# A two-layer graph network with residual and normalisation: rows of x split by way of a PSUM bank, VectorE's instructions in program order in the setup, and earlier due times for the last blocks

## The chip, the cores and the metric

The kernel runs on one core of one Trainium2 chip. The metric is device time in microseconds of one execution, the median over several runs; the profile is of one further execution.

## The reference

The inputs are x (12,500 nodes of 256 features, float32), 200,000 edges (src, dst), sorted by dst, and the weights of two graph layers and of an output layer. The edges are not spread evenly: dst is 12,500 times the square of a uniform number, so the low nodes have many edges and the high ones few.

```python
def _sage_conv(x, src, dst, W_l, b_l, W_r):
    msgs = x[src]
    agg = jax.ops.segment_sum(msgs, dst, num_segments=N_NODES)
    deg = jax.ops.segment_sum(jnp.ones((src.shape[0],), x.dtype), dst, num_segments=N_NODES)
    mean = agg / jnp.maximum(deg, 1.0)[:, None]
    return mean @ W_l + b_l + x @ W_r
...
    h = jax.nn.relu(_sage_conv(x, src, dst, W1_l, b1, W1_r))
    h = jax.nn.relu(_sage_conv(h, src, dst, W2_l, b2, W2_r))
    return h @ W3 + b3
...
    x = _layernorm(x + _L0_gnn_ref(x, edge_index, ...), axis=-1)
```

## The kernel before

**Two ways to sum the messages.** The 12,500 nodes make 98 blocks of 128 rows, and the 200,000 edges make 1,563 tiles of 128. For the "hot" nodes (the first 5 x 256 in layer 1, the first 7 x 256 in layer 2) the kernel counts how often each source occurs for each target (`count`, L677) and multiplies the count matrix with all rows of the table (`product`, L654). The rows are float32 and the products bf16, so each row is split in three bf16 parts that add up to it: `x3_d` holds the parts of x, `h3_d` those of layer 1's output h. For the "cold" nodes the rows of the edges' sources are gathered from memory: one gather (L257) is an indirect DMA of 128 rows, issued by GpSimd (POOL), and four gathers make a round. TensorE (PE) sums the round's rows by a one-hot matrix (the strips, `part_ps`, L269), ScalarE (ACT) copies the sum out (`some`, L279), a second small product places it (`sum_ps`, L285), and VectorE (DVE) adds it to a ring of eight blocks of sums (L299). Four buffers `got` hold the rows of four rounds, so POOL can be at most four rounds ahead of the strips.

**Stages.** The setup (L301 to L546) loads src and dst, turns them edge by edge into the tables that the gathers and the one-hot matrices need, and tests the data against what the plan of the program assumes. `by_sorting` is a slower program that runs if a test fails; the branch is taken at the very end (L45), by a flag that is written to memory (L988) and loaded again (L41). Layer 1 has 269 rounds (1,076 gathers from x), layer 2 has 247 (988 gathers from h).

**The order.** The order on PE and POOL is written out by hand (`manual_schedule`, L445); the framework's scheduler orders the instructions of DVE, ACT and SP. `layer` (L584) does it: in each round it issues four gathers and their strips, adds what the round before gave, and in three parts of the round works on finished blocks (`pieces`) and on the dense work (`fill`). The dense work has estimated costs, and `due` (L623) spreads it over all rounds but the last eight. In layer 1 its first stage is the count of the first 256 nodes together with the split of x (`splits`, L803, one `split_rows` for each of the 98 blocks); after it come the products of the groups, each beside the count of the next. A block of 128 nodes is finished when all edges that can fall into it have been summed; `left_after` (L236) tells it from `at_least` (L94), which allows the data to be SLACK = 8 tiles from the square law. A finished block goes to a queue, where at most two are worked on, in three pieces in layer 1 (`first_block`, L913) and five in layer 2 (`last_block`, L939), two turns apart. The blocks of a dense group go to the same queue when its product is done (L800).

**The split before.** `split_rows` (L648) loads a block of x, and `exact` (L637) makes the parts: DVE subtracts the upper bf16 half of x from x (L643, into `rest`), and the upper half of the rest from the rest (L644, the third part); ACT copies the two upper halves (L645, L646); SP stores the three parts (L652). All of it lies in SBUF. `exact` is also used for h in `first_block` (L935).

Of the kernel before, what the change touches and what calls it, by code (L numbers as in the profile page):

```python
# [7 lines left out]
F32 = mybir.dt.float32  # L8
# [15 lines left out]
P = 128  # L24
# [3 lines left out]
def kernel(tc, x, src, dst, w1l, b1, w1r, w2l, b2, w2r, w3, b3, out):  # L28

    args = (x, src, dst, w1l, b1, w1r, w2l, b2, w2r, w3, b3, out)
    flag = tc.nc.dram_tensor("unfit_d", (1, 1), I32).ap()
    by_runs(tc, *args, flag)
    with tc.tile_pool(name="flag", bufs=1) as pool:
        unfit_i = pool.tile([1, 1], I32, name="unfit_i")  # L40
        tc.nc.sync.dma_start(unfit_i, flag)  # L41
        unfit = tc.nc.values_load(
            unfit_i[0:1, 0:1], min_val=0, max_val=1,
            skip_runtime_bounds_check_because="it is clamped to 0..1 where it is made")
    with tc.If(unfit > 0):  # L45
        by_sorting(tc, *args)
# [3 lines left out]
def by_runs(  # L50
# [36 lines left out]
    FAR = 1 << 20  # L87
    SLACK = 8
    RB = 8
    RN = RB * P  # L90
    assert D % P == 0 and E % 2 == 0 and G * W == P


    def at_least(t):  # L94
        return N * (max(t - SLACK, 0) / NT) ** 2 - 2

    def at_most(t):
        return N * ((t + SLACK) / NT) ** 2 + 2

# [201 lines left out]
    with tc.tile_pool(name="setup", bufs=1) as su, \  # L301
            tc.tile_pool(name="setup_ps", bufs=2, space=PSUM) as su_ps:
        def edges(a, first, name, fill):
# [14 lines left out]
            return t  # L318

        src_i = edges(src, 0, "src_i", 0)  # L320
        dst_i = edges(dst, 0, "dst_i", FAR)
# [9 lines left out]
        whole = (NT // G) * G  # L331
        with nc.allow_non_contiguous_dma(reason="one edge of each tile"):
            nc.scalar.dma_start(f4_i[:, :NT // G], dst[0:whole * P].rearrange(
                "(g j l) -> j g l", j=G, l=P)[:, :, 0])
            if NT > whole:
                left = NT - whole
                nc.scalar.dma_start(
                    f4_i[0:left, NT // G:NG],
                    dst[whole * P:whole * P + (left - 1) * P + 1:P][:, None])
            nc.scalar.dma_start(f8_i, dst[lows[HG1] * P:PAIRS * P].rearrange(  # L340
                "(g j l) -> j g l", j=G, l=2 * P)[:, :, 0])
            nc.scalar.dma_start(f1_i, dst[None, 0:HC * P * P:P])
            nc.scalar.dma_start(fours_i, dst[0:P * P:P * G][:, None, None].to_broadcast([P // G, G, 1]))
            for c in range(C0, PAIRS // P):
                nc.scalar.dma_start(pair_i[:, c:c + 1], dst[c * P * P:(c + 1) * P * P:2 * P][
                    :, None, None].to_broadcast([P // 2, 2, 1]))

# [15 lines left out]
        nc.vector.tensor_copy(lanes_5[:, :, :LW // 5], steps_f[:, :LW].rearrange("p (a b) -> p a b", a=5))  # L363
        nc.vector.tensor_copy(steps_7[:, :, :NB // 7], steps_f[:, :NB].rearrange("p (a b) -> p a b", a=7))


# [65 lines left out]
        nc.vector.tensor_copy(within_f, within)  # L432
        nc.vector.tensor_scalar(lo2, after, within_f, None, op0=OP.add)

        for g in got:

            nc.vector.memset(g[:, :, D:D + 1], 1.0)
        nc.vector.memset(sums, 0.0)
        nc.vector.memset(degs, 0.0)
        nc.vector.memset(ones, 1.0)  # L440
        nc.vector.memset(ones_b, 1.0)
        nc.vector.memset(zeros_b, 0.0)

# [13 lines left out]

        nc.vector.tensor_copy(steps, steps_f)
        bits = su.tile([P, HC, P], I32, name="bits")
        low = su.tile([P, HC, P], F32, name="low")  # L460
        nc.vector.tensor_scalar(bits, src_i[:, :HC], P - 1, None, op0=OP.bitwise_and)
        nc.vector.tensor_copy(low, bits)
# [4 lines left out]
        start = su.tile([P, HC], F32, name="start")  # L467
        nc.vector.tensor_copy(start[:, 0:1], fours_i)
        nc.vector.tensor_copy(start[:, 1:], first[:, 1:HC])
        f1 = su.tile([1, HC * P], F32, name="f1")  # L470
        nc.vector.tensor_copy(f1, f1_i)
        off_f = su.tile([1, HC * P], F32, name="off_f")
        nxt_first = su.tile([P, HC], F32, name="nxt_first")
        nc.vector.tensor_copy(nxt_first, nxt_i[:, :HC, P - 1])
        most_c = max(b - a for a, b in spans)
# [20 lines left out]
        nxt_f = su.tile([P, CH, P], F32, name="nxt_f")  # L496
        nc.vector.tensor_copy(nxt_f, nxt_i)
        nc.vector.scalar_tensor_tensor(scr, dst_f, 0.0, nxt_f, op0=OP.add, op1=OP.is_gt,
# [10 lines left out]
        for sign in (-1, 1):  # L509
            law = su.tile([1, NG], F32, name="law", bufs=2)  # L510
            nc.vector.tensor_scalar(law, fours, float(G) / NT, float(sign * SLACK) / NT,
                                    op0=OP.mult, op1=OP.add)
            nc.vector.tensor_scalar(law, law, 0.0, None, op0=OP.max)
# [69 lines left out]

    def layer(gathers, block, n_pieces, dense, dense_cost):  # L584

# [35 lines left out]
        for i in range(i0, n + 1):  # L621
            before = gathers.step()
            due = dense_cost * min(1.0, (i + 1 - i0) / (n - i0 - 8))  # L623
            for part in range(3):
                if part == 2 and before:
                    gathers.summed(*before, done)
                    while begun < left_after(before[0]):
                        waiting.append((begun,))
                        begun += 1
                pieces()  # L630
                fill(spent + (due - spent) / (3 - part))
# [3 lines left out]


    def exact(t, s, rest):  # L637


        def upper(a):  # L640
            return a.bitcast(BF16).rearrange("p (n h) -> p n h", h=2)[:, :, 1]

# [3 lines left out]
        nc.scalar.copy(s[:, 1], upper(rest))  # L646
# [156 lines left out]
    def splits():  # L803
        for b in range(NB):
            split_rows(b)
            yield COST_SPLIT
# [551 lines left out]
```

## Time and profile before

| | us |
|---|---|
| runs | 2829.16, 2819.84, 2829.44 (median 2829.16) |
| the profiled execution | 2817.42, its span 2815.6 |
| PE busy | 2321.8 (82%) |
| POOL busy | 2014.5 (72%) |
| DVE busy | 1525.3 (54%) |
| ACT busy | 1098.5 (39%) |
| mean granted clock of TensorE | 0.928 |

The span runs from the first to the last instruction. POOL's instructions are nearly all gathers: 1,076 from x of 997 ns in the mean, and 988 from h of 951 ns, and between two of them some 0.30 us lie in which POOL issues the next. [...]

### The profile page before, as it was taken

The page shows a single profiled execution, that of the slowest core. Times are in us where ns is not written, and L with a number is a line of the kernel's source. Part 1 is how long each engine was busy: PE and PEld are TensorE (multiplying, and loading weights), DVE is VectorE, ACT ScalarE, POOL GpSimd, SP SyncE. Part 2 cuts the span into 40 slices and gives each one's busy share as a digit, 9 for nine tenths or more (in the row PEclk, how much of TensorE's full clock was granted, in tenths as well). Part 3 has the DMA queues.
Part 4 walks back from the last instruction along what each step waited for, and adds up shares of the span by engine and source line. Part 5 has one row for each costly group of instructions (what it writes and reads, how often), then busy time and mean ns, then how long its engine had stood idle before and what let it go on. Part 6 is the DMA issues. An engine that isn't in the chain of part 4 may idle for free. (4 is left out here: it accounts for less than half of the span.)

```text
span 2815.6 us, 54531 instructions
## 1 busy us (share of the span) xinstructions
PE 2321.8 (82%) x18268; PEld 1594.5 (57%) x18268; DVE 1525.3 (54%) x5362; ACT 1098.5 (39%) x2270; POOL 2014.5 (72%) x2074
## 2 busy tenths in 40 slices
PE   3466668988988999999985787778788889999995
PEld 1122225656656766767753565556566666677773
DVE  5688886755655676676662134443233344444443
ACT  0433675655554565565551123342111122222222
POOL 5767677777777777777775777777777767777771
PEclk9977778999989999999999999999899999999997
DMA  4467679869859879868855777777889889888872
GB/s 115 137 202 221 191 219 306 265 193 315 272 183 329 268 234 305 266 194 268 263 167 167 233 249 223 225 228 251 273 282 302 286 282 303 284 264 271 270 241 65
DMA packets 420983, 676.56 MB, mean 240 GB/s; under 512 B 72419, under 2 KB 279385, under 8 KB 420697
## 3 DMA queue, kind: packets, MB, share of 16 engines
q1 hardware_dynamic: 316807, 401.13, 43.7%
q0 software_dynamic: 99072, 270.66, 31.2%
q8 instruction: 150, 2.46, 0.4%
q10 hardware_dynamic: 4818, 1.19, 0.3%
q14 instruction: 136, 1.11, 0.1%
HBM read 582.84 MB, written 89.92 MB: 239 GB/s over the span
## 5 line engine op out<-in xcount | busy, mean ns | idle before, releaser
L257 POOL DMA_INDIRECT got<-in_x_dram,src_t x1076 | 1072.4, 997 | 401.3 <-issue 281.5
L257 POOL DMA_INDIRECT got<-h_d,src_t x988 | 940.0, 951 | 343.7 <-issue 258.7
L667 PE MATMUL dense_ps<-counts,rows 128*128 128x256 bf16 x7056 | 954.0, 278 | 93.6 <-DMA rows<-h_d 53.2
L667 PEld LDWEIGHTS <-rows 128*128 128x128 bf16 x7056 | 671.2, 99 | 316.9 <-issue 84.2
L735 ACT CAST counts<-count_ps 128x686 f32 (+2 forms) x620 | 539.8, 871 | 246.7 <-PE count_ps L729 188.0
L269 PE MATMUL part_ps<-got,one 128*32 128x257 f32 (+1 forms) x4128 | 362.8, 425 | 161.7 <-DMA got<-h_d,src_t 107.6
L729 PE MATMUL count_ps<-pick,low 128*128 128x490 bf16 (+2 forms) x1052 | 320.8, 358 | 57.7 <-DVE low L694 32.0
L691 DVE TENSOR_SCALAR pick<-steps,key_t 128x686 bf16<-128x686 f16 (+2 forms) x748 | 301.1, 405 | 57.6 <-PE count_ps L729 43.0
L213 DVE TENSOR_TENSOR one<-lo_t,lane_b 128x128 f32<-128x128 bf16 x516 | 147.3, 285 | 313.7 <-PE part_ps L269 310.4
L279 ACT COPY some<-part_ps 128x257 f32<-128x257 f32 (+1 forms) x361 | 134.3, 372 | 421.6 <-PE part_ps L269 420.8
L694 DVE TENSOR_SCALAR low<-lanes,low_t 128x130 bf16<-128x130 f16 x748 | 201.7, 271 | 93.7 <-PE count_ps L733 91.9
L269 PEld LDWEIGHTS part_ps<-got,one 128*32 128x32 f32 x4128 | 86.9, 112 | 275.5 <-issue 219.9
L285 PE MATMUL sum_ps<-two,some 128*128 128x128 f32 x1444 | 239.9, 292 | 2.0 <-DVE sums L299 1.9
L892 ACT COPY sums<-zero 128x256 f32<-128x256 f32 x172 | 69.4, 403 | 412.1 <-PE block_ps L889 410.2
L299 DVE TENSOR_TENSOR sums<-sums,sum_ps 128x256 f32 x361 | 148.3, 411 | 145.4 <-PE sum_ps L285 112.7
L285 PEld LDWEIGHTS sum_ps<-two,some 128*128 128x128 f32 x1444 | 208.7, 204 | 16.6 <-issue 9.1
L729 PEld LDWEIGHTS <-low 128*128 128x128 bf16 x1052 | 104.3, 100 | 159.4 <-DVE low L694 61.5
L895 DVE TENSOR_TENSOR own<-block_ps,biases 128x256 f32<-128x256 f32 x196 | 82.7, 422 | 191.7 <-PE block_ps L889 188.4
L863 ACT COPY own_t<-block_ps 128x256 f32<-128x256 f32 x294 | 108.9, 372 | 128.4 <-PE block_ps L861 127.2
L699 DVE TENSOR_SCALAR aft<-steps,after_t 128x98 bf16<-128x98 f16 x621 | 155.9, 251 | 0.0
L898 ACT ACTIVATE h<-own 128x256 f32<-128x256 f32 x196 | 81.6, 416 | 149.6 <-DVE own L896 146.7
L733 PE MATMUL count_ps<-aft,low 128*128 128x98 bf16 x614 | 133.7, 218 | 0.0
(179 smaller groups left out, 2454.6 us busy)
## 6 DMA issues: line engine op xcount, KB each, us to landing
rows<-h_d SPq DMA_DIRECT2D x343, 384.0 KB
rows<-x_d SPq DMA_DIRECT2D x245, 384.0 KB
count_d<-counts SPq DMA_DIRECT2D x28, 896.0 KB
counts<-count_d SPq DMA_DIRECT2D x28, 896.0 KB
x_sb<-in_x_dram SPq DMA_DIRECT2D x194, 128.0 KB
x_d<-parts SPq DMA_DIRECT2D x98, 192.0 KB
h_d<-parts SPq DMA_DIRECT2D x98, 192.0 KB
got<-in_x_dram,src_t POOLq DMA_INDIRECT x1076
```

The lines of the kernel that those rows point to most:

```text
L213: nc.vector.tensor_tensor(one, lo[:, a:a + n * (G - 1) + 1:n].unsqueeze(2).to_broadcast([P, G, W]), lane_b[:, :W].unsqueeze(1).to_broadcas ...
L257: rows = nc.gpsimd.indirect_dma_start(out=g[:, j, :D], out_offset=None, in_=self.table, in_offset=bass.IndirectOffsetOnAxis(ap=src_t[:, e: ...
L269: strip = nc.tensor.matmul(part_ps[j * W:(j + 1) * W, :width], lhsT=one[:, j], rhs=g[:, j, :width], start=r == 0, stop=r == n - 1)
L279: nc.scalar.copy(some[:, :width], part_ps[:, :width])
L285: nc.tensor.matmul(sum_ps[:, c], lhsT=some[:, c * P:(c + 1) * P], rhs=two, start=True, stop=True)
L299: nc.vector.tensor_add(own, own, sum_ps[:, :NC])
L667: nc.tensor.matmul(ps[:, c], lhsT=rows[:, b % 2, k, c * P:(c + 1) * P], rhs=c_sb[:, b, :DN], start=False, stop=b == NB - 1 and k == 2 and ...
L691: nc.vector.tensor_scalar(r[:, :w * NB], steps[:, :w * NB], key_t[g][:, t - lo_g:t - lo_g + 1], None, op0=OP.is_equal)
L694: nc.vector.tensor_scalar(low.rearrange("p (a b) -> p a b", a=5), lanes_5[:, :, :LW // 5], low_t[:, t:t + 1], None, op0=OP.is_equal)
L699: nc.vector.tensor_scalar(aft.rearrange("p (a b) -> p a b", a=7), steps_7[:, :, :NB // 7], after_t[g][:, t - lo_g:t - lo_g + 1], None, op0 ...
L729: nc.tensor.matmul(c[:, a * NB:b * NB], lhsT=s, rhs=r[:, a * NB:b * NB], start=True, stop=alone)
L735: nc.scalar.copy(to[:, :, bass.ds(off_act.at(t), w)], c.rearrange("p (d s) -> p s d", s=NB))
```

## The change

It has four parts.

- **The split** (`split_rows`): ACT copies the loaded block into half a PSUM bank (two blocks share a bank of `dense_pool`, which the products do not use in this stage), DVE subtracts the upper half of x from it in place, ACT copies the two upper halves, one from SBUF and one from PSUM. The third part (the subtraction of the second part from the rest) and the store of the block follow at the beginning of the next block's split. `exact` stays for h.
- **The setup**: from the loads of the edges to the table `lo2`, DVE executes in the program's order; the memsets stand ahead of the tables, the loads of `pair_i` ahead of the other small loads on ACT's queue; and some DVE operations that are not needed for the first gathers wait for `lo2` (`later`).
- **The last blocks**: the slack is 8 tiles up to tile NT - 64, then 5, and 3 for the last 16 tiles, and the test of the data follows it; `due` spreads the dense work of layer 2 over all rounds but the last 14, and in the rounds after that everything that is left of it is due at once.
- **The flag** is a tile in SBUF, made ahead of layer 2, and each engine reads it there.

```diff
     args = (x, src, dst, w1l, b1, w1r, w2l, b2, w2r, w3, b3, out)
-    flag = tc.nc.dram_tensor("unfit_d", (1, 1), I32).ap()
-    by_runs(tc, *args, flag)
     with tc.tile_pool(name="flag", bufs=1) as pool:
-        unfit_i = pool.tile([1, 1], I32, name="unfit_i")
-        tc.nc.sync.dma_start(unfit_i, flag)
+        flag = pool.tile([1, 1], I32, name="flag")
+        by_runs(tc, *args, flag)
         unfit = tc.nc.values_load(
-            unfit_i[0:1, 0:1], min_val=0, max_val=1,
+            flag[0:1, 0:1], min_val=0, max_val=1,
...
-    SLACK = 8
+
+    SLACKS = [(0, 8), (NT - 64, 5), (NT - 16, 3)]
...
+    def slack(t):
+        return [by for since, by in SLACKS if since <= t][-1]
+
     def at_least(t):
-        return N * (max(t - SLACK, 0) / NT) ** 2 - 2
+        return N * (max(t - slack(t), 0) / NT) ** 2 - 2
...
+        in_order = ExitStack()
+        in_order.enter_context(tc.manual_schedule(engines={DVE}))
         src_i = edges(src, 0, "src_i", 0)
...
+            for c in range(C0, PAIRS // P):
+                nc.scalar.dma_start(pair_i[:, c:c + 1], dst[c * P * P:(c + 1) * P * P:2 * P][
+                    :, None, None].to_broadcast([P // 2, 2, 1]))
             nc.scalar.dma_start(f4_i[:, :NT // G], dst[0:whole * P].rearrange(
...
+        for g in got:
+
+            nc.vector.memset(g[:, :, D:D + 1], 1.0)
+        nc.vector.memset(sums, 0.0)
+        nc.vector.memset(degs, 0.0)
...
-        nc.vector.tensor_scalar(lo2, after, within_f, None, op0=OP.add)
...
+        first_tables = nc.vector.tensor_scalar(lo2, after, within_f, None, op0=OP.add)
+
+        in_order.close()
+
+        def later(op):
+
+            tc.add_manual_dep(op.ins, first_tables.ins.name, LANDED, reason="the first gathers' tables")
...
-        nc.vector.tensor_copy(steps, steps_f)
+        later(nc.vector.tensor_copy(steps, steps_f))
...
-            due = dense_cost * min(1.0, (i + 1 - i0) / (n - i0 - 8))
+
+            due = dense_cost * (i + 1 - i0) / (n - i0 - left) if i + 1 < n - left else 1e8
...
+    split = []
+
     def split_rows(b):
+
+
+        if split:
+            left, s, at, bank = split.pop()
+            nc.vector.tensor_tensor(s[:, 2], left, s[:, 1], op=OP.subtract)
+            nc.sync.dma_start(x3_d[:, at], s)
+        if b == NB:
+            return
+        if b % 2 == 0:
+            bank = dense_pool.tile([P, NC, DN], F32, name="dense_ps")
         t = load_rows(x, N, b, "split_sb")
         s = work.tile([P, 3, D], BF16, name="parts")
-        exact(t, s, work.tile([P, D], F32, name="rest", tag="own"))
-        nc.sync.dma_start(x3_d[:, b], s)
+        left = bank[:, b % 2]
+        nc.scalar.copy(left, t)
+        leaves = nc.vector.tensor_tensor(left, left, upper(t), op=OP.subtract)
+        if b < 3:
+            later(leaves)
+        nc.scalar.copy(s[:, 0], upper(t))
+        nc.scalar.copy(s[:, 1], upper(left))
+        split.append((left, s, b, bank))
...
-        layer(gathers_1, first_block, 3, staged(stages_1), cost_of(stages_1))
+        layer(gathers_1, first_block, 3, staged(stages_1), cost_of(stages_1), 8)
...
-    layer(Gathers(h_d, True), last_block, 5, staged(stages_2), cost_of(stages_2))
...
-        unfit = su.tile([1, 1], I32, name="unfit")
-        nc.vector.tensor_scalar(unfit, n_bad, 1.0, None, op0=OP.min)
-        nc.sync.dma_start(flag, unfit)
+        nc.vector.tensor_scalar(flag, n_bad, 1.0, None, op0=OP.min)
+
+    layer(Gathers(h_d, True), last_block, 5, staged(stages_2), cost_of(stages_2), 14)
```

More of the change, by code (lines that the diff above doesn't have):

```diff
@@ L91, in by_runs @@
     assert D % P == 0 and E % 2 == 0 and G * W == P
+    def slack(t):
+        return [by for since, by in SLACKS if since <= t][-1]
     def at_least(t):
-        return N * (max(t - SLACK, 0) / NT) ** 2 - 2
+        return N * (max(t - slack(t), 0) / NT) ** 2 - 2
     def at_most(t):
-        return N * ((t + SLACK) / NT) ** 2 + 2
+        return N * ((t + slack(t)) / NT) ** 2 + 2
     HG1, HG, DN = 5, 7, 256
@@ L343, in by_runs @@
             nc.scalar.dma_start(fours_i, dst[0:P * P:P * G][:, None, None].to_broadcast([P // G, G, 1]))
-            for c in range(C0, PAIRS // P):
-                nc.scalar.dma_start(pair_i[:, c:c + 1], dst[c * P * P:(c + 1) * P * P:2 * P][
-                    :, None, None].to_broadcast([P // 2, 2, 1]))
         diff = su.tile([P, P], I32, name="diff")
@@ L364, in by_runs @@
         nc.vector.tensor_copy(steps_7[:, :, :NB // 7], steps_f[:, :NB].rearrange("p (a b) -> p a b", a=7))
+        for g in got:
+            nc.vector.memset(g[:, :, D:D + 1], 1.0)
+        nc.vector.memset(sums, 0.0)
+        nc.vector.memset(degs, 0.0)
+        nc.vector.memset(ones, 1.0)
+        nc.vector.memset(ones_b, 1.0)
+        nc.vector.memset(zeros_b, 0.0)
         def columns(t, cs, to, name, t0=0, a=None, b=None):
@@ L432, in by_runs @@
         nc.vector.tensor_copy(within_f, within)
-        nc.vector.tensor_scalar(lo2, after, within_f, None, op0=OP.add)
[L435 to L442, printed above, removed]
+        first_tables = nc.vector.tensor_scalar(lo2, after, within_f, None, op0=OP.add)
+        in_order.close()
+        def later(op):
+            tc.add_manual_dep(op.ins, first_tables.ins.name, LANDED, reason="the first gathers' tables")
         ctx.enter_context(tc.manual_schedule(engines={PE, POOL}))
@@ L453, in by_runs @@
         early_round()
-        nc.vector.tensor_copy(steps, steps_f)
+        later(nc.vector.tensor_copy(steps, steps_f))
         bits = su.tile([P, HC, P], I32, name="bits")
         low = su.tile([P, HC, P], F32, name="low")
-        nc.vector.tensor_scalar(bits, src_i[:, :HC], P - 1, None, op0=OP.bitwise_and)
+        later(nc.vector.tensor_scalar(bits, src_i[:, :HC], P - 1, None, op0=OP.bitwise_and))
         nc.vector.tensor_copy(low, bits)
@@ L467, in by_runs @@
         start = su.tile([P, HC], F32, name="start")
-        nc.vector.tensor_copy(start[:, 0:1], fours_i)
+        later(nc.vector.tensor_copy(start[:, 0:1], fours_i))
         nc.vector.tensor_copy(start[:, 1:], first[:, 1:HC])
         f1 = su.tile([1, HC * P], F32, name="f1")
-        nc.vector.tensor_copy(f1, f1_i)
+        later(nc.vector.tensor_copy(f1, f1_i))
         off_f = su.tile([1, HC * P], F32, name="off_f")
         nxt_first = su.tile([P, HC], F32, name="nxt_first")
-        nc.vector.tensor_copy(nxt_first, nxt_i[:, :HC, P - 1])
+        later(nc.vector.tensor_copy(nxt_first, nxt_i[:, :HC, P - 1]))
         most_c = max(b - a for a, b in spans)
@@ L496, in by_runs @@
         nxt_f = su.tile([P, CH, P], F32, name="nxt_f")
-        nc.vector.tensor_copy(nxt_f, nxt_i)
+        later(nc.vector.tensor_copy(nxt_f, nxt_i))
         nc.vector.scalar_tensor_tensor(scr, dst_f, 0.0, nxt_f, op0=OP.add, op1=OP.is_gt,
@@ L510, in by_runs @@
             law = su.tile([1, NG], F32, name="law", bufs=2)
-            nc.vector.tensor_scalar(law, fours, float(G) / NT, float(sign * SLACK) / NT,
-                                    op0=OP.mult, op1=OP.add)
+            for since, by in SLACKS:
+                c = -(-since // G)
+                later(nc.vector.tensor_scalar(law[:, c:], fours[:, c:], float(G) / NT,
+                                              float(sign * by) / NT, op0=OP.mult, op1=OP.add))
             nc.vector.tensor_scalar(law, law, 0.0, None, op0=OP.max)
@@ L582, in by_runs, with layer @@
     MOST, APART = 2, 2
-    def layer(gathers, block, n_pieces, dense, dense_cost):
+    def layer(gathers, block, n_pieces, dense, dense_cost, left):
         queue, waiting, done = [], [], set()
@@ L634, in layer, with upper @@
             pieces()
+    def upper(a):
+        return a.bitcast(BF16).rearrange("p (n h) -> p n h", h=2)[:, :, 1]
     def exact(t, s, rest):
-        def upper(a):
-            return a.bitcast(BF16).rearrange("p (n h) -> p n h", h=2)[:, :, 1]
         nc.vector.tensor_tensor(rest, t, upper(t), op=OP.subtract)
@@ L803, in splits @@
     def splits():
-        for b in range(NB):
+        for b in range(NB + 1):
             split_rows(b)
```

## The prediction

> **What bounds the kernel.** I read first the span cut into stretches, engine by engine, with POOL's count of gathers, then POOL's own waits, then the timeline at the three places where POOL is idle.
>
> ```profile
> 140.00:420.00 280.00, 186.35 (x964) 75.84 (x964) 245.57 (x866) 147.18 (x350) 199.23 (x193) 0.72 0.70 208
> 300.00:420.00 120.00, 84.24 (x453) 37.27 (x446) 103.47 (x422) 92.52 (x205) 90.70 (x89) 0.72 0.74 220
> 700.00:1400.00 700.00, 655.05 (x5736) 469.14 (x5735) 441.02 (x1656) 397.01 (x738) 521.84 (x537) 0.97 0.80 257
> 1502.00:1900.00 398.00, 302.00 (x2368) 209.10 (x2368) 142.25 (x477) 106.98 (x189) 301.55 (x317) 0.92 0.72 227
> ```
>
> The columns are the stretch, its length, then busy time and instructions of PE, its weight loads, DVE, ACT and POOL, the granted clock, DMA share and GB/s. From 1502 to 1900 a gather takes 301.55/317 = 0.951 us, and one is issued each 398/317 = 1.256 us: POOL does nothing but write descriptors and issue. From 700 to 1400 the pitch is 1.304 us, from 140 to 420 it is 1.451 us. 2,064 gathers at 1.256 us make 2592 us of the span of 2815.6. So POOL is the bound, and what can be won lies in the other 223 us: the start, the slow pitch of the first dense stage, the gap between the layers, and the tail.
>
> ```profile
> 19.47 1.97 PE L373 MATMUL src_ps<-ident,src_f 128*128 128x128 f32 x8 [19.47 <-DVE ident L361]
> 23.99 0.17 DVE L390 CAST begin<-pair_i 128x6 f32<-128x6 int32 x1 [4.44 <-DMA w1l_sb<-in_L_gnn_W_l_dram]
> 26.85 1.10 POOL L257 DMA_INDIRECT got<-in_x_dram,src_t  x1 [24.05 <-DVE src_t L376]
> ...
> 1501.29 0.94 POOL L257 DMA_INDIRECT got<-h_d,src_t  x1 [24.83 <-DMA h_d<-parts]
> ...
> 2759.22 0.95 POOL L257 DMA_INDIRECT got<-h_d,src_t  x1 [0.30 <-issue]
> ...
> 2787.65 1.03 PE L884 MATMUL block_ps<-w2l_sb,d_sb 128*128 128x256 f32 x4
> ...
> 2799.98 0.42 DVE L958 TENSOR_TENSOR z<-block_ps,x_sb 128x256 f32<-128x256 f32 x1 [3.64 <-PE block_ps L956]
> ...
> 2802.95 0.24 SPq L41 DMA_DIRECT2D unfit_i<-unfit_d  x1
> ```
>
> In the timeline (start, length, what, and the idle time before it with its releaser) the first gather waits until 26.85, layer 2's first gather waits 24.83 us for the last blocks of layer 1, and after the last gather come 56.4 us. The blocks with d_sb, those of the last dense group, are the very last work.
>
> **Part 1, the start.** The source rows are in SBUF at 10.2 (their conversion starts at 10.22, ends at 11.05), but their transposition waits until 19.47 for ident, which DVE made at 19.21, behind memsets, index work and a wait for f4. In program order ident is made in the first 3 us. The transposes then start at 11.1; the first four take half of 1.97, 1.0 us; the first half of src_t 0.65: the first gather starts near 13.1, 13.7 us earlier. That is the upper end. The added wait: all DVE work behind the conversion of dst now stands in order, and the dst load's last part is issued at 17.54, so this chain can start at about 19.6. Before, DVE then stood still for 4.44 us until 23.99 at L390, with ident's and the transposes' work behind it; pair_i now leads ACT's queue, and this wait goes. The two-thirds of the setup after that are DVE work with small idle times until 65, and POOL has only four rounds of buffers, so it will wait where its earlier gathers meet strips that DVE's keys hold up; 65 to 95 was held by the gathers and moves with them. The lower end is the 4.44 us of one wait, less the 1.4 us in which other operations used it: 3. I take 10, nearer the upper end, since the setup's second half waited for gathers. What ACT issues later now (f4, eight microseconds to land) is needed by lo2, which DVE reached at 36.9: covered. The wait of the `later` operations for lo2 holds 2.5 us of DVE conversions and the keys behind them, which before came from 38.8 on; lo2 should come by 34, so nothing is late. **-10** (-14 to -3).
>
> **Part 2, the split.** 98 splits between 96.7 and 437.5, one each 3.5 us.
>
> ```profile
> L643 DVE TENSOR_TENSOR rest<-split_sb 128x256 f32<-128x256 f32 x98 | 40.5, 413 | 20.1 <-DMA split_sb<-in_x_dram 13.4 <-ACT parts L646 5.8 <-ACT counts L735 0.9
> L645 ACT COPY parts<-split_sb 128x256 bf16<-128x256 bf16 x98 | 39.8, 406 | 62.0 <-DMA x_d<-parts 39.0 <-DMA split_sb<-in_x_dram 10.7 <-DMA h_d<-parts 7.7
> L863 ACT COPY own_t<-block_ps 128x256 f32<-128x256 f32 x294 | 108.9, 372 | 128.4 <-PE block_ps L861 127.2
> L895 DVE TENSOR_TENSOR own<-block_ps,biases 128x256 f32<-128x256 f32 x196 | 82.7, 422 | 191.7 <-PE block_ps L889 188.4
> ```
>
> These groups end with busy time, mean ns, and idle time with its releasers. DVE keeps two subtractions; with one operand in PSUM they cost 422 ns (L895) against 413: +0.9 us for 98 pairs. ACT gets a third copy: into PSUM no row shows, between 372 (from PSUM) and 406 ns, and the one that now reads PSUM gains up to 34: +0.37 us each, 36 us in all. From 300 to 420 ACT is busy 92.5 of 120 us (77%); 35 splits there add 13, which makes 88%. It fits, but behind an ACT copy that waits stand the evacuations of the counts (L735), then PE's strips, then POOL's buffers. DVE, 86% busy there, is unchanged. The gain: a gather takes 199.23/193 = 1.032 us here against 0.951 where DVE does little, 81 ns x 193 = 15.6 us, which is all that the subtractions can be slowing POOL's descriptors by, and the count's own DVE operations take a share.
>
> [...]
>
> [...]
>
> Loss from below: 36 us, if every new ACT copy comes to lie on PE's path. I take -5, a third of the POOL row, because both engines have idle time. **-5** (-15.6 to +36).
>
> **Part 3, the gap between the layers.** Following the queue's rule turn by turn with the two slacks: at the last round block 95 still had a piece to go, with 96 and 97 behind it; now it is done a round earlier. Its piece cost PE 1487.04 to 1490.6, 3.5 us; the deg rows' trip through memory for 96 and 97 (1486.93 to 1494.1) stays. **-3** (-5 to 0).
>
> **Part 4, layer 2's pace.** 239 rounds of dense work become 233, 2.6% more in each. POOL's waits for strips in layer 2 are 24.7 us in all (the gathers from h, releaser PE L269). Between nothing and a doubling; I take 2. **+2** (0 to +25).
>
> **Part 5, the tail.** The same walk: before, the last group's product is only taken as done after the last round, so its two blocks queue behind 97, and 22 turns follow the last round. Now the product ends at round 232, its blocks are finished by round 237, and 10 turns follow. The residual additions z stand at 2780.89, 2783.61, 2790.51, 2793.22 and 2799.98, for blocks 95, 96, 97 and the two dense ones. Block 96 had turn 753 before and has it now; 97 follows one turn later. So the last z falls at about 2783.6, 16.4 earlier; 95 has two pieces less and 97 comes after 96 by its own work. **-17** (-20 to -10).
>
> **Part 6, the flag.** After the last store of rows (2802.15) come the flag's load at 2802.95, its landing, a branch of 3.7 us on SP's queue, and the end at 2815.6. The store, load and landing go (2804.4 - 2802.5: 2 us); POOL, idle since 2760, may be through its own part earlier, at most 4 more. The test of the flag costs 0.5 us of PE and DVE ahead of layer 2, beside other blocks' work. **-4** (-6 to -2).
>
> **Sum.** -10 - 5 - 3 + 2 - 17 - 4 = -37 against the profiled 2817.42: 2780.4. That execution was 11.7 us below the median of the runs; the middle of all four executions is 2824.5, and I set the forecast there: **2787.5**.
>
> **Rivals.** (A) *The start does not carry.* DVE paces the first stage (246 of 280 us busy), so POOL's early gathers only wait at the fifth round: part 1 is 3, part 2 nothing: -25, 2799. (B) *More comes of it.* The first stage is POOL's, the subtractions were all of its slowness: -13.7 - 15.6 - 3 - 17 - 4 = -53, 2771. Against it: the count's picks run in the same stretch. (C) *The tail stays.* If the blocks' order is not as I walked it, 3, 5 and the 2 of part 4 fall away: -19, 2805.5. For my walk speaks that the d_sb blocks are last in the trace. (D) *Slower: ACT paces the first stage.* Each split now goes ACT, DVE, ACT, DVE, and its store is issued a block later, with two buffers for the parts; ACT's 39.0 us of waits for x_d<-parts could double. If the copies' 36 and another 39 us lie on PE's path, 75 us replace the -5: +43, 2867. It decides from 32/98 = 0.33 us per split on. Against it: ACT's 23% of idle time.
>
> **Numbers.** Forecast 0.48, A 0.20, B 0.13, C 0.10, D 0.09. The forecast's own range is 2774 to 2798. The range 2760 to 2813 leaves out D, the lower edge of B and the upper of C. A measurement of this kernel tells 0.5% from no change: below 2815.0 is faster, above 2843.3 slower. All of the forecast, A and B and most of C are faster: 0.87; the rest of C and the mild end of D 0.05; slower 0.08.
>
> **What will show it.** First gather near 13 us; POOL's time per gather in the first stage under 1.0 us and the number of gathers by 420 us up by eight or more; the gap between the layers near 22 us; last z some 20 us after the last gather, with no d_sb row behind it. Wrong would be: strips that wait for ACT's parts, an ACT over 90% busy before 420, more waits for x_d<-parts.

## The result, and the profile after

The changed kernel takes 2856.96 us (median of six runs, 2846.92 to 2867.55), the kernel before 2829.06 us beside it: a ratio of 1.0108, 95% interval 1.008 to 1.0136. The forecast was 2787.5. The profiled execution has a span of 2851.3 us, against 2815.6.

The span is laid out along POOL, as the prediction did it. In the timeline of the changed kernel (start, length, engine, line and operation; in brackets the idle time before it and its releaser):

```profile
11.32 1.10 POOL L259 DMA_INDIRECT got<-in_x_dram,src_t  x1 [8.53 <-DVE src_t L390]
...
428.16 0.11 PEld L689 LDWEIGHTS <-zeros_b 128*128 128x128 bf16 x1
...
429.69 0.95 POOL L259 DMA_INDIRECT got<-in_x_dram,src_t  x1 [0.30 <-issue]
...
501.64 0.42 DVE L669 TENSOR_TENSOR parts<-dense_ps,parts 128x256 bf16<-128x256 f32 x1 [0.44 <-ACT parts L683]
...
502.12 0.59 PE L689 MATMUL dense_ps<-counts,zeros_b 128*128 128x512 bf16 x1 [73.45 <-DVE parts L669]
...
505.31 0.94 POOL L259 DMA_INDIRECT got<-in_x_dram,src_t  x1 [74.67 <-PE part_ps L271]
...
1558.12 0.94 POOL L259 DMA_INDIRECT got<-h_d,src_t  x1 [21.65 <-DMA h_d<-parts]
...
2818.04 0.94 POOL L259 DMA_INDIRECT got<-h_d,src_t  x1 [0.30 <-issue]
...
2841.41 0.42 DVE L990 TENSOR_TENSOR z<-block_ps,x_sb 128x256 f32<-128x256 f32 x1
```

The reader is to see the two brackets with 73 and 74 us. At 428 TensorE comes to the first matmul of the first product (L689), and it stands there until 502: it waits for the third part (L669) of the last block of x. The strips (L271) are behind it in PE's order, the four `got` buffers are full, and POOL stands as well. Everything else went the way the change meant it:

| | before | after | difference |
|---|---|---|---|
| first gather | 26.85 | 11.32 | -15.5 |
| gathers of layer 1, first to last | 1448.7 | 1524.2 | +75.5 |
| gap between the layers | 24.83 | 21.65 | -3.2 |
| gathers of layer 2 | 1257.9 | 1259.9 | +2.0 |
| last gather to the end of the span | 56.4 | 33.3 | -23.1 |
| span | 2815.6 | 2851.3 | +35.7 |

The stretches of the changed kernel (the columns are those of the prediction's first view):

```profile
140.00:420.00 280.00, 185.32 (x965) 78.39 (x964) 226.85 (x805) 154.75 (x381) 185.75 (x193) 0.72 0.63 186
300.00:420.00 120.00, 82.38 (x412) 33.80 (x404) 96.63 (x378) 95.97 (x228) 74.69 (x79) 0.69 0.72 210
...
430.00:505.00 75.00, 2.88 (x16) 1.11 (x16) 23.20 (x65) 24.11 (x70) 0.64 (x1) 0.51 0.62 194
```

From 430 to 505 TensorE is busy for 2.9 of 75 us and POOL issues one gather; but DVE and ACT are busy for a third of the time only. So this is not an engine that is full, it is a chain in which each waits for the other, or for a block on its way to or from memory. From 140 to 420 a gather takes 185.75/193 = 0.962 us instead of 1.032, as was hoped, and yet there are 193 gathers as before.

The engines' waits over the whole span (total us, times, longest):

```profile
PE dense_ps L689 <- DVE parts L669: 73.4, 1, 73.4
ACT parts L682 <- DMA x_d<-parts: 63.5, 38, 5.2
ACT dense_ps L678 <- DVE parts L669: 47.0, 43, 11.5
DVE parts L669 <- ACT parts L683: 42.6, 36, 5.8
```

And the groups of the new split's operations (busy time, mean ns, idle time with its releasers):

```profile
L679 DVE TENSOR_TENSOR dense_ps<-dense_ps,split_sb 128x256 f32<-128x256 f32 x98 | 41.8, 426 | 27.5 <-ACT dense_ps L678 27.0
L669 DVE TENSOR_TENSOR parts<-dense_ps,parts 128x256 bf16<-128x256 f32 x98 | 40.9, 417 | 43.4 <-ACT parts L683 42.6
...
L678 ACT COPY dense_ps<-split_sb 128x256 f32<-128x256 f32 x98 | 38.1, 389 | 47.7 <-DVE parts L669 47.0 <-DMA split_sb<-in_x_dram 0.6
L683 ACT COPY parts<-dense_ps 128x256 bf16<-128x256 bf16 x98 | 36.3, 370 | 31.9 <-DVE dense_ps L679 31.9
```

The operations cost what the prediction took from its rows (ACT's new copy 389 ns, 372 to 406 forecast). The waits between them are what is new. One block in the stretch where nothing else runs shows the chain:

```profile
498.17 0.42 DVE L669 TENSOR_TENSOR parts<-dense_ps,parts 128x256 bf16<-128x256 f32 x1
...
498.63 0.38 ACT L678 COPY dense_ps<-split_sb 128x256 f32<-128x256 f32 x1 [0.49 <-DVE parts L669]
...
499.04 0.43 DVE L679 TENSOR_TENSOR dense_ps<-dense_ps,split_sb 128x256 f32<-128x256 f32 x1 [0.44 <-ACT dense_ps L678]
499.50 0.37 ACT L683 COPY parts<-dense_ps 128x256 bf16<-128x256 bf16 x1 [0.17 <-DVE dense_ps L679]
...
499.90 0.42 DVE L669 TENSOR_TENSOR parts<-dense_ps,parts 128x256 bf16<-128x256 f32 x1 [0.44 <-ACT parts L683]
...
500.36 0.38 ACT L678 COPY dense_ps<-split_sb 128x256 f32<-128x256 f32 x1 [0.49 <-DVE parts L669]
```

ACT, DVE, ACT, DVE, and only then ACT's copy of the next block: 1.73 us per block, although two blocks in turn lie in different halves of the bank. Both copies above wait 0.49 us for the subtraction in the other half, and over the whole stage 43 of the 98 copies wait for it, 47.0 us in all. For every second block the program gives a sufficient reason: there a new tile of the one-buffer `dense_pool` begins, and the old one must be free in both halves. The copy at 500.36 is that of the last block, the second of its tile, and waits all the same; why it does was not shown.

In the 73.4 us 22 blocks were stored, 3.34 us each; so the bare chain is 38 us of it, and most of the rest are ACT's waits for the buffers of the parts (26.9 us for x_d<-parts between 428 and 503).

### The profile page after: what moved, and what is told of

Its sections match the earlier page's. It is cut to its first block, busy times and chain, and to the rows that moved or that the text cites. A ratio compares the mean times of both kernels' runs of the same rounds, so it can differ in the third digit from the quotient of the medians.

```text
span 2851.3 us, 54521 instructions
## 1 busy us (share of the span) xinstructions
PE 2319.9 (81%) x18268; PEld 1595.3 (56%) x18268; DVE 1538.7 (54%) x5366; ACT 1128.5 (40%) x2368; POOL 2001.2 (70%) x2074
## 4 chain that ended last, share of the span: by engine, by line
PE 46%; DMA 23%; POOL 11%; issue 8%; DVE 7%; ACT 3%; DVEq 0%; SPq 0%; ACTq 0%; POOLq 0%
PE dense_ps L699 17%; POOL got L259 11%; PE part_ps L271 6%; DMA got<-h_d,src_t 5%; PE block_ps L916 5%; PE count_ps L761 4%; DMA rows<-h_d 4%; PE block_ps L921 4%; PE sum_ps L287 4%; DMA got<-in_x_dram,src_t 3%; DMA x_sb<-in_x_dram 3%; DMA rows<-x_d 3%; DMA x_d<-parts 2%; PE block_ps L988 2%; PE block_ps L893 2%
## 5 line engine op out<-in xcount | busy, mean ns | idle before, releaser
L259 POOL DMA_INDIRECT got<-in_x_dram,src_t x1076 | 1057.8, 983 | 475.9 <-issue 280.0
L271 PE MATMUL part_ps<-got,one 128*32 128x257 f32 (+1 forms) x4128 | 361.8, 424 | 165.2 <-DMA got<-h_d,src_t 107.2
L271 PEld LDWEIGHTS part_ps<-got,one 128*32 128x32 f32 x4128 | 86.9, 112 | 278.7 <-issue 217.3
```

The source lines that it names most:

```text
L259: rows = nc.gpsimd.indirect_dma_start(out=g[:, j, :D], out_offset=None, in_=self.table, in_offset=bass.IndirectOffsetOnAxis(ap=src_t[:, e: ...
L271: strip = nc.tensor.matmul(part_ps[j * W:(j + 1) * W, :width], lhsT=one[:, j], rhs=g[:, j, :width], start=r == 0, stop=r == n - 1)
```

## The experiments

**Theory S** says: the splits go one after the other through one bank, so the compiled order of DVE sets them later; when TensorE comes to the first product, which needs that bank, some are left, and it stands until they are done. In DVE's compiled order 97 of the 98 third parts stand ahead of the last count that precedes the product in the kernel before, and 75 in the changed one (in its trace one more, 76, is done when TensorE comes, so 22 are left). Its rivals: the start made the splits late (T), ACT's third copy paces (A), the deferred store with two buffers does it (D), and others below.

These runs were on four chips. On three of them every kernel, the one before too, is 17 to 19% slower than in the first runs; so ratios and differences on one chip count, and the absolute times that were expected were off there. "Stands" is the time for which PE stood at the first product's first matmul, "left" the blocks whose parts were not stored by then.

| run | before, us | this, us | ratio (95%) | ahead | stands, us | left |
|---|---|---|---|---|---|---|
| the change | 2829.06 | 2856.96 | 1.0108 (1.008 to 1.0136) | 75 | 73.4 | 22 |
| e1_old_split | 3356.44 | 3325.11 | 0.9913 (0.988 to 0.9945) | 97 | none | 1 |
| e2_split_alone | 3356.44 | 3420.13 | 1.0199 (1.0157 to 1.0241) | 79 | 67.8 | 19 |
| e3_left_sbuf | 3356.44 | 3322.75 | 0.9909 (0.9879 to 0.9939) | 96 | 0.5 | 1 |
| e4_same_block | 3356.44 | 3405.91 | 1.0147 (1.0105 to 1.0188) | 75 | 73.6 | 22 |
| e5_before_again | 3317.26 | 3313.01 | one run | 97 | 0.5 | 1 |
| e6_changed_again | 3317.26 | 3353.36 | 1.0115 (1.0087 to 1.0142) | 75 | 76.4 | 22 |
| e7_odd_sbuf | 3317.26 | 3286.69 | 0.9922 (0.9898 to 0.9946) | 96 | none | 1 |
| e8_more_parts | 3317.26 | 3348.34 | one run | 76 | 70.8 | 21 |
| e9_product_later | 2819.83 | 2801.81 | 0.9936 (0.9905 to 0.9967) | 97 | none | 0 |
| e10_sooner_in_program | 2819.83 | 2873.20 | one run | 48 | 106.1 | 43 |
| e11_start_only | 2819.83 | 2791.69 | 0.9904 (0.9866 to 0.9942) | 97 | 0.3 | 1 |
| e12_tail_only | 2819.83 | 2793.51 | 0.9913 (0.9882 to 0.9944) | 97 | none | 1 |
| e13_old_split_again | 3312.29 | 3281.42 | 0.9899 (0.9875 to 0.9924) | 97 | 0.5 | 1 |
| e14_changed_again | 3312.29 | 3362.87 | 1.0155 (1.0126 to 1.0184) | 75 | 76.3 | 22 |
| e15_odd_sbuf_again | 3312.29 | 3284.05 | 0.9922 (0.9895 to 0.9949) | 96 | none | 1 |

### Which part of the change it is

e1_old_split takes the new split out and leaves the rest:

```diff
-        left = bank[:, b % 2]
-        nc.scalar.copy(left, t)
-        leaves = nc.vector.tensor_tensor(left, left, upper(t), op=OP.subtract)
+        rest = work.tile([P, D], F32, name="rest", tag="own")
+        leaves = nc.vector.tensor_tensor(rest, t, upper(t), op=OP.subtract)
...
+        nc.vector.tensor_tensor(s[:, 2], rest, upper(rest), op=OP.subtract)
         nc.scalar.copy(s[:, 0], upper(t))
-        nc.scalar.copy(s[:, 1], upper(left))
-        split.append((left, s, b, bank))
+        nc.scalar.copy(s[:, 1], upper(rest))
+        nc.sync.dma_start(x3_d[:, b], s)
```

> The changed kernel with the split of before (in SBUF, third part and store in the same block); start, boundary, tail and flag as changed. Theory S (the splits' way through the one bank ends late, and the first product, which needs that bank, holds TensorE's queue and with it the gathers): the 74.7 us gap before a gather at 505 us is gone, no gap of a gather over 12 us in the first stage, the first gather stays near 11.3 us and the last z near 23 us nearer to the end; 2829.1 - 15.5 - 3.2 + 2 - 23 = about 2789 us (2780 to 2798). In the compiled order of DVE's instructions 97 of 98 third parts stand ahead of the last pick before the first product, as in the kernel before; in the changed kernel 75. Rival T (DVE's written-out order at the start made the splits late): the gap stays, 2845 us or more.

e2_split_alone is the kernel before with the new `split_rows` and nothing else.

> The kernel before with the new split alone. Theory S: 79 of 98 third parts stand ahead of the last pick before the first product in DVE's compiled order, so 19 splits are left when TensorE comes to the product; at the 3.1 us per split of the changed kernel's gap (73.5 us for 23 to 24) that is one gap of about 59 us and a time near 2829 + 59 = 2888 us (2870 to 2900). POOL's time per gather between 100 and 400 us falls to about 0.96 us as in the changed kernel. Rival T (the start's order is the cause): no such gap, 2815 to 2835 us.

Without the new split the kernel is 31 us faster than before and PE does not stand; with the new split alone it is 64 us slower, and PE stands for 67.8 us with 19 blocks left (59 was expected, at 3.1 us a block; it was 3.57). The start is not the cause, so T falls. That chip's own pace spoiled the absolute figures of e1: 31 us under the kernel before where 40 was expected.

### What in the split it is

e3_left_sbuf keeps ACT's third copy and the deferred third part, and only moves the remainder out of the bank:

```diff
-        if b % 2 == 0:
-            bank = dense_pool.tile([P, NC, DN], F32, name="dense_ps")
...
-        left = bank[:, b % 2]
+        left = work.tile([P, D], F32, name="rest", tag="own")
```

> The changed kernel, but the remainder lies in an SBUF buffer (the one that the split of before used) instead of the PSUM bank; ACT's copy of x into it, the subtraction in place, and the third part a block later are kept. Theory S: the product's bank is free, 96 of 98 third parts stand ahead of the product in DVE's order, no gap over 12 us in the first stage, about 2789 us (2780 to 2800), and POOL's time per gather in the first stage is back at 1.0 us and more, because DVE reads two SBUF operands again. Rival A (ACT's third copy per split paces the stage): the time stays near 2857 us. Rival D (the deferral, with two buffers for the parts): near 2857 us as well.

e4_same_block keeps the bank and undoes the deferral: the last two lines stand at the end of the same block's split.

```diff
         nc.scalar.copy(s[:, 1], upper(left))
-        split.append((left, s, b, bank))
+        nc.vector.tensor_tensor(s[:, 2], left, s[:, 1], op=OP.subtract)
+        nc.sync.dma_start(x3_d[:, b], s)
```

> The changed kernel, split by way of the bank, but the third part and the store in the same block instead of a block later. Theory S: 75 of 98 third parts stand ahead of the product in DVE's order as in the changed kernel, the gap of 65 to 80 us at the first product stays, 2850 to 2865 us. Rival D (the deferral holds the two buffers of the parts and makes the splits late): the gap shrinks below 25 us and the time falls below 2810 us.

e8_more_parts keeps both and adds a third buffer for the parts:

```diff
-        s = work.tile([P, 3, D], BF16, name="parts")
+        s = work.tile([P, 3, D], BF16, name="parts", bufs=3)
...
-            low = work.tile([P, LW], BF16, name="low", bufs=6)
+            low = work.tile([P, LW], BF16, name="low", bufs=5)
```

> The changed kernel with three buffers for the bf16 parts instead of two (and five instead of six for the low-bit masks, to make room). 76 of 98 third parts stand ahead of the product in DVE's order. Theory S (the chain through the one bank, one block at a time, is what is slow): the gap stays at 60 to 80 us. Rival D (stores that hold the two buffers of the parts make the splits late): the gap falls under 35 us.

With the remainder in SBUF PE does not stand, though ACT copies three times and the store comes a block later: A and D as the deferral fall. With the bank it stands 73.6 us even without the deferral, and 70.8 us with a third buffer (76.4 in the changed kernel beside it): D as the buffers falls too. So it is the bank that makes PE stand.

How long it stands is not set by the bank alone. The third buffer takes away ACT's waits for the stores, and the waits for the loads of x come in their place. While PE stands, in e6_changed_again (468 to 545):

```profile
ACT parts L682 <- DMA x_d<-parts: 23.7, 12, 5.2
...
ACT parts L682 <- DMA split_sb<-in_x_dram: 1.1, 1, 1.1
```

and in e8 (472 to 544):

```profile
ACT parts L682 <- DMA split_sb<-in_x_dram: 31.5, 14, 5.5
...
ACT parts L682 <- DMA x_d<-parts: 0.8, 1, 0.8
```

So about half of the stand is the chain, and the other half is waiting for the blocks' transfers, which a third buffer only moves from the stores to the loads.

e5_before_again and e6_changed_again are the two kernels unchanged, profiled on one chip:

> The kernel before, unchanged, profiled beside the others, so that spans can be laid against it on the same chip: the first gather near 26.5 us, the first product's first matmul with 97 splits stored, no gap over 12 us in the first stage. On the chip of the first four runs its time was 3356 us, not 2829 us; the theories speak of differences to it.

> The changed kernel, unchanged. Theory S (late splits in the product's bank hold TensorE's queue): the gap at the first product of 70 to 80 us, and 25 to 55 us above the kernel before on the same chip, as the same split with the third part in its own block (49 us above). If it lies under the kernel before here, the chip decides, and the theory is not enough.

The change costs nearly the same there: first gather 15.6 us earlier, layer 1 76.7 longer, gap 2.2 shorter, layer 2 3.6 shorter, end 18.5 shorter, in all +36.8 between the two spans.

### Use of the bank, or splits that are late?

e7_odd_sbuf sends only the even blocks through the bank and splits the odd ones in SBUF:

```diff
-        if b % 2 == 0:
-            bank = dense_pool.tile([P, NC, DN], F32, name="dense_ps")
...
+        if b % 2 == 0:
+            left = dense_pool.tile([P, NC, DN], F32, name="dense_ps")[:, 0]
...
+        else:
+            left = work.tile([P, D], F32, name="rest", tag="own")
```

> The changed kernel, but only the even blocks of x go by way of the bank (third part a block later, as changed); the odd ones are split in SBUF as before. 96 of 98 third parts stand ahead of the product in DVE's compiled order. Theory S (what counts is whether the chain through the bank is done when the product comes, not that the bank is used): no gap over 12 us at the first product, about 30 to 45 us under the kernel before; POOL's mean time per gather between 100 and 400 us lies between the 0.97 us of the bank and the 1.03 us of SBUF. Rival B (any use of the product's bank by the splits holds the product): a gap of 30 us or more, at or above the kernel before.

e9_product_later leaves all 98 splits in the bank and moves the first product:

```diff
     def dense(g, table3, c_sb, waiting, with_deg):
+        if g == 0 and with_deg:
+            for _ in range(40):
+                yield COST_DENSE
```

> The changed kernel, all 98 splits by way of the bank, but the first product begins 40 of its steps later in the program (it gives way 40 times before its first matmul), so that 97 of 98 third parts stand ahead of it in DVE's compiled order instead of 75. Theory S (TensorE's queue stands at the product until the late splits have left its bank): the gap of 70 to 80 us is gone, none over 15 us at the product, and the time is 20 to 45 us under the kernel before on the same chip. Rival P (the 75 us are work of the splits that has to be done at some time, wherever the product stands): the gap shrinks but the time comes back as smaller gaps before it, and the time stays above the kernel before.

In e7 the bank is used 49 times and nothing stands: using the bank is not the fault. In e9 all blocks go through it, and moving the product by 40 of its steps is enough: nothing stands, and the kernel is 18 us faster than the one before instead of some 28 slower (28 on the first chip; the changed kernel itself was not run on this one). That is 2 us less than the lower end expected. Something of the price is left, as is seen beside e11_start_only on the same chip, which has the split of before (and other due times, see below). In the stretches of e9:

```profile
420.00:500.00 80.00, 49.97 (x243) 22.07 (x243) 57.70 (x225) 56.69 (x136) 46.45 (x49) 0.69 0.86 267
...
600.00:1400.00 800.00, 747.12 (x6601) 535.75 (x6601) 491.78 (x1841) 439.81 (x825) 602.39 (x616) 0.96 0.82 263
```

and of e11:

```profile
420.00:500.00 80.00, 65.59 (x490) 40.31 (x489) 54.03 (x229) 48.15 (x93) 54.70 (x56) 0.90 0.91 289
...
600.00:1400.00 800.00, 735.93 (x6467) 524.59 (x6466) 498.60 (x1874) 448.46 (x836) 604.03 (x620) 0.96 0.80 257
```

Seven gathers fewer from 420 to 500 and four fewer from 600 to 1400, where PE is busy for 11 us more: some of the price comes back elsewhere, as P had it (layer 1's gathers take 1473.0 us against 1453.6), but about a quarter of it, not all.

One thing was not tried: a bank for the splits that the product does not need. In e3 and e7 the splits are no longer late, and in e9 the product comes later; no run has late splits and a free bank.

e10_sooner_in_program was meant to give a dose, with the splits dealt out twice as fast among the counts of the program:

```diff
-                parts.append((splits(), NB * COST_SPLIT))
+                parts.append((splits(), 0.5 * NB * COST_SPLIT))
```

> The changed kernel with the splits dealt out twice as fast among the counting in the program. In DVE's compiled order only 48 third parts then stand ahead of the product, not 75: 50 are left. Theory S: the gap grows with what is left; 23 left gave 74.7 and 77.5 us, 3.2 to 3.4 us each, so 50 left give 160 to 170 us (140 to 190), and the time is near 120 us above the kernel before on the same chip (95 to 145). Rival Q (the gap is a fixed price of the bank changing hands between splits and product): the gap stays at 70 to 80 us.

Dealt out sooner, the splits stand *later* against the product in the compiled order (why was not shown; the smaller cost also changes how much of the stage falls to a round). PE stands longer, as S says and Q does not, but 106.1 us, not 140 to 190, and the time is 53 us above the kernel before, not 120. Its waits between 425 and 531 show where the difference lies:

```profile
PE dense_ps L689 <- DVE parts L669: 106.1, 1, 106.1
...
ACT parts L682 <- DMA x_d<-parts: 26.6, 14, 7.7
```

beside those of the changed kernel between 428 and 503:

```profile
PE dense_ps L689 <- DVE parts L669: 73.4, 1, 73.4
...
ACT parts L682 <- DMA x_d<-parts: 26.9, 12, 5.2
```

43 blocks were left, 2.47 us each, against 22 at 3.34. ACT's waits for the stored parts are the same 27 us in both. Without them a block costs 1.85 and 2.11 us, near the bare chain's 1.73: so in these two traces the price is a chain per block plus a sum of waits that does not grow with the blocks. The 32.7 us more of standing cost only some 25 us more of time (one run, on another chip); 316 gathers were issued before the product here, not 284.

### The other parts alone, and all of it on one chip

e12_tail_only has the slack, the due times and the flag. e11_start_only was meant to be the kernel before with the setup's new order and nothing else, but its kernel keeps more of the change, against the kernel before:

```diff
-    SLACK = 8
+    SLACKS = [(0, 8), (NT - 64, 5), (NT - 16, 3)]
...
-            due = dense_cost * min(1.0, (i + 1 - i0) / (n - i0 - 8))
+            due = dense_cost * (i + 1 - i0) / (n - i0 - left) if i + 1 < n - left else 1e8
```

The flag's tile in SBUF is in it too, written by a DMA at the end; and `left`, which `layer` is no longer given, is a variable of the setup, NT - 1560 = 3, so the dense work is spread over all rounds but the last three. It is the start with part of the tail's change, not the start alone.

> The kernel before with the start alone (DVE in the program's order up to the first tables, the loads' new order, what is sent behind). If the earlier start carries to the end: first gather near 11.3 us and 10 to 18 us under the kernel before. If it does not carry (the first stage is paced by other work): within 5 us of it.

> The kernel before with the narrower slack, the due times of the dense work and the flag alone. By the traces of before and after: the time from the last gather to the end falls by 18 to 23 us, the gap between the layers by 2 to 3 us, so 17 to 28 us under the kernel before. If the last blocks' work only moves to in front of the last gather: within 8 us of it, with the second layer's gathers longer by what the end is shorter.

e11 is 28 us faster than the kernel before (interval 16 to 38), e12 26 us (16 to 33). In e12's trace the time from the last gather to the end of the span is 32.7 us against 56.4 in the first profile, the gap between the layers 22.2 against 24.8, both as expected, and layer 2's gathers are not longer (1252.8 against 1257.9).

In e11's trace the first gather is 15.5 us earlier and layer 1's gathers take 4.9 us more, so 10.6 us carry to the end of layer 1. That is what the start's own lines show, near the lower end of the 10 to 18 us expected, and it is no sharp figure: layer 1 of e12, without the new start, took 5.9 us more than in the first profile as well. The other 17.7 us by which this execution is shorter than the first profile are 9.4 behind the last gather (47.0 against 56.4), 7.4 in layer 2 and 0.9 in the gap. The 9.4 us lie where the narrower slack and the due times work, which e11 has; what the 7.4 us are is open. What the start alone is worth in the whole time was not measured.

> The changed kernel with the split of before, once more, on another chip if it falls so. If the other parts of the change carry as their own lines in the trace say (start 15.5, boundary 3, end 23 us, second layer 2 us longer): 35 to 45 us under the kernel before where a gather's round takes as long as in the first trace; where each matmul follows its data 10 us and more later (as on the chip of the first four runs), 25 to 40 us under it. If the start's and the end's gains add up as measured one by one (28 and 26 us): 50 to 58 us under it.

> The changed kernel on the same chip as the run before it: TensorE stands 70 to 78 us at the first product with 22 splits left, and the kernel is 68 to 85 us above the one with the split of before, 25 to 45 us above the kernel before.

> Even blocks by way of the bank, odd ones in SBUF, on the same chip as the two others. If shorter gathers in the first stage (0.03 us each over some 200 gathers, 6 us) carried through, 4 to 8 us under the version with the split of before; if the first stage is paced by other work, the same within 4 us.

The bank's split costs 3362.87 - 3281.42 = 81 us on this chip, with 76.3 us of standing. The stretch from 140 to 420 of e13, then of e14, then of e15:

```profile
140.00:420.00 280.00, 180.65 (x866) 73.49 (x870) 219.75 (x769) 128.24 (x309) 179.54 (x175) 0.65 0.62 187
```

```profile
140.00:420.00 280.00, 171.37 (x860) 71.43 (x860) 207.17 (x720) 130.40 (x326) 168.24 (x176) 0.69 0.55 165
```

```profile
140.00:420.00 280.00, 175.68 (x848) 73.89 (x848) 217.06 (x755) 136.04 (x339) 172.32 (x173) 0.66 0.62 185
```

A gather takes 1.026 us with the split in SBUF, 0.956 through the bank and 0.996 with half of each, and in 280 us there are 175, 176 and 173 of them. The shorter gathers do not become more gathers, and e15 is no faster than e13. The best ratios, near 0.99, belong to the versions without the bank (e1, e3, e13); e7 and e15 are not to be told from them. The 28 and 26 us of e11 and e12 are not to be added, since e11 has part of the tail's change; on two slower chips start and end together gave 31 us (e1, e13), and on a chip of the first kind they were not run together without the bank.

## Why the prediction was wrong, point by point

- **Part 2, the split: the step that failed.** It said -5, "-15.6 to +36", and bounded the loss by "36 us, if every new ACT copy comes to lie on PE's path". Here it is some +75 (layer 1's gathers; 64 us for the split alone in e2, 81 between e13 and e14). The bound priced the new operations, and those were priced right (389 and 370 ns on ACT, 426 and 417 on DVE). It did not ask who needs the bank next. The product of the following stage takes the same `dense_pool` bank, with one buffer; before, it needed only the first blocks' stored parts to begin, now it needs the last block's. And it took the 98 splits to keep their places in DVE's order, where a chain of four steps through one bank moved 22 of them behind the product. e3, e7 and e9 each take away one side of this and the stand is gone.
- **The gain in part 2** was real in each gather and nothing in the end: 0.962 against 1.032 us per gather, but 193 gathers from 140 to 420 in both kernels. At 428 the changed kernel was 8 gathers ahead (282 to 274), which is what it was ahead at 60 already (31 to 23). In between the lead had grown to 18 (199 to 181 at 300) and went again: 79 gathers from 300 to 420, against 89. POOL's waits for strips took what the shorter gathers gave: 51.5 us between 100 and 430, against 33.4 in the same stage before. Rival A had said this of the first stage.
- **Rival D** had the chain, the deferred store and the buffers, and its forecast for the waits for x_d<-parts (39.0 us doubled) came near: 63.5. Its price of 2867 is close to 2857 by another mechanism: ACT paced nothing (95.97 of 120 us from 300 to 420), and without the deferral (e4) or with a third buffer (e8) PE stands almost as long.
- **Part 1, the start**: the first gather is at 11.32, not near 13.1, since the conversion of the source rows starts at 8.39 and not at 10.22. What carries is near the value taken: at 428 eight gathers are worth 8 x 1.25 = 10 us; in e11, with the split of before, four (278 to 274), but 10.6 us at the end of layer 1. One reading was wrong: in the trace before, ident (19.21) and the first transposes (19.47) stand ahead of the wait of 4.44 us that ends at 23.99; src_t stands behind it.
- **Part 3, the gap**: -3.2 for -3. **Part 4, layer 2's pace**: +2.0 for +2.
- **Part 5, the tail**: the last z comes 23.4 us after the last gather, 40.8 before: -17.4 for -17, so rival C falls. **Part 6, the flag**: from the last z to the end 9.9 us for 15.6: -5.7 for -4.

All parts but the split come to -40 here (-15.5 - 3.2 + 2.0 - 23.1), or -34 with the 10 us that carry, close to the -32 forecast for them; e1 and e13, which have these parts and the split of before, measured -31 on slower chips. The signs of failure that the prediction had named were an ACT over 90% busy, strips that wait for ACT's parts, and more waits for x_d<-parts; only the last showed, and none was the cause. The one to name was an engine with a fixed order that comes to a buffer which its last user still holds.

## What to carry to other kernels

When a tile is borrowed "because nobody uses it in this stage", price the handing back: here the first matmul of the next owner waited 73.4 us for the last use, and all that stood behind it in PE's fixed order waited too (from 430 to 505 PE was busy for 2.9 us). Work whose order a scheduler chooses is not where the program puts it (here 75 of the 98 third parts stood ahead of the product instead of 97); after an edit that adds a serial chain, count in the compiled order how much of it is left when the engine with the hand-written order needs the result. And a faster instruction on an engine that is not what paces the stage gave only longer waits here: a gather of 0.962 us instead of 1.032, 193 gathers from 140 to 420 in both kernels, and 51.5 us of POOL's waits for strips instead of 33.4.

## What the runs showed of the hardware

- **POOL's gathers and DVE's operands.** With DVE's 196 subtractions reading one operand from PSUM instead of two from SBUF, a gather between 140 and 420 is 0.070 us shorter in two pairs of traces (1.032 to 0.962; 1.026 to 0.956) and 0.030 shorter with half of the blocks moved. Over all traces it is 1.011 to 1.053 us with the subtractions in SBUF (1.016 in e3, which keeps ACT's third copy) and 0.956 to 0.979 with all of them by way of the bank. The 0.070 us make 193 x 0.070 = 13.5 us over the 193 gathers between 140 and 420. How the subtractions' operands and the gathers hang together was not shown. Nor was what POOL does while a gather is busy: "write descriptors" in the prediction is its author's reading of the 0.951 us.
- **Chips.** The kernel before took 2829 us in the first runs, 2820 us on one of the four later chips, and 3356, 3317 and 3312 us on the three others. Its gathers on one of the three are as short as in the first profile, but POOL waits longer ahead of them. The page's two groups of gathers in the first profile (busy, mean ns, idle before):

```profile
L257 POOL DMA_INDIRECT got<-in_x_dram,src_t x1076 | 1072.4, 997 | 401.3 <-issue 281.5
L257 POOL DMA_INDIRECT got<-h_d,src_t x988 | 940.0, 951 | 343.7 <-issue 258.7
```

and in e5_before_again, the same program:

```profile
L257 POOL DMA_INDIRECT got<-in_x_dram,src_t x1076 | 1065.6, 990 | 660.7 <-issue 261.4
L257 POOL DMA_INDIRECT got<-h_d,src_t x988 | 937.9, 949 | 586.7 <-issue 249.1
```

  The idle time grows by 259 and 243 us, which is about the whole difference of the spans (3311.2 - 2815.6 = 496). The mean granted clock of TensorE is 0.879 there, 0.928 in the first profile. In the traces' packets the rows of a gather land as soon there (the last packet 3.2 us after the gather's start in the median, 3.5 in the first profile), but in all but 5% of the rounds the last strip's matmul starts more than 10 us after them, where in the first profile a twentieth of the rounds start within 0.8 us. What delays it was not settled.
